# Even and odd blocks in two halves: the overlap-add of a block convolution with three additions instead of five, one PSUM pool, and channel pairs side by side

## The chip, the cores and the metric

The kernel runs on one core of one Trainium2 chip. The metric is the time of one execution on the device in microseconds (us). Three runs of the kernel before gave 13579.16, 13577.97 and 13587.48 us; their median is 13579.16 us.

## What is computed

The input x holds 32 images of 128 channels and 32 x 32 pixels; an image read as a sequence has L = 1024 positions. Two residual layers follow each other. Only the front part of the first layer is touched here:

```python
u = group_norm(x).reshape(B, S, L)                  # B = 32, S = 128
h = jnp.einsum('bdl,de->ble', u, W_enc) + b_enc     # 1024 model channels
K = 2.0 * jnp.einsum('dn,dnl->dl', Cc * Bd, vand).real   # 64 taps per model channel
y = irfft(rfft(z, n) * rfft(K, n), n)[..., :L]      # z is h with axes swapped: a causal convolution
y = gelu(y + D[:, None] * z)
```

So each of the 1024 model channels of each image is encoded from 128 input channels, and then convolved along its 1024 positions with a filter of 64 taps that belongs to that channel (D is folded into the first tap). After that the first layer has a gated linear unit, a layer norm and a decoder, and the second layer a deformable convolution. Those later parts are one long block of the program; the change does not touch them.

## The kernel before

The program runs three parts in a row: a small table of filters (`ssm_kernel_table`), the encoder and convolution (`ssm_convolution`), and the main block (`main_block`). The convolution's result `y_d` goes to device memory and the main block reads it back.

`ssm_convolution` walks over 8 groups k of 128 model channels. For each k it calls `encode(k)` and then `convolve(k, z)`. The instructions of each engine stand in the order in which these functions call them (`manual_schedule`)[...].

**Encoding.** For each of the 32 images, `image(b, u)` makes two halves g of four position blocks (128 positions each). A half is four matmuls (L223) with a block of the normalised image `u` as the stationary operand and the encoder's weights as the moving one. Their results lie in a PSUM tile `psz` of one bank. One VectorE addition (L227) adds the bias and writes the half into `z[g]`, laid out as position, channel, block, image. The innermost run of that write is one element: neighbouring channels lie NB x B = 128 elements apart. `psz` has two buffers. For k = 0 the group norm of the images runs inside the same loop (`group_norm_steps`, L161 to L180), spread over ScalarE, TensorE and VectorE in steps; the loads, the storing of `u_d` (L250) and the encoding of image t-3 stand between them. For k > 0 the normalised images are loaded back from `u_d` (L236).

**Convolution.** A convolution with 64 taps of a 128-position block is a matmul with a banded table `toe` of 192 columns (TW). The result's positions stand in reverse: its first RW = 64 columns run over into the next block, the other 128 are the block itself. In `convolve` the stationary operand is the half i of `z` for one channel, 128 positions by 128 columns (4 blocks x 32 images); the result has these 128 block-image rows as partitions. Channels are taken in groups of 8 (`CG`), with one load of `toe` each (L281), and inside a group in quads of four (`QC`). For each quad and each half i there are

- four matmuls into a PSUM tile `psy` of two banks (L299),
- a ScalarE copy of the overlapping columns into `t` (L307),
- VectorE additions that carry the overlap to the block that follows (L311): 64 rows and 32 rows inside the half, and for i = 1 another 32 rows that come from half 0, so five for the two halves,
- a ScalarE gelu that evacuates the tile into `yo` (L320).

The gelu of a tile isn't called at once: it goes on the list `waiting`, and `finish()` calls it after the next tile's copy and additions have been called. After the second quad of a group, `store` joins the same list: eight DMAs of 128 KB by GpSimd's queue (L332). The pool of `psy` has three buffers of two banks, and the group norm's small results take their tiles from that pool as well.

With blocks split into a first half (0 to 3) and a second half (4 to 7), ordered by `ORDER = (0, 2, 1, 3)`, the block that follows another one lies in the same half, except at one place. The order makes the carries contiguous in partitions.

```python
                        carry(64, 64, over[0:64])
                        carry(32, 32, over[64:96])
                        if i > 0:
                            carry(0, 32, last[96:P])
                        finish()
```

[...]two buffers of one bank and three of two are eight banks.

Of the kernel before, what the change touches and what calls it, by code (L numbers as in the profile page):

```python
# [7 lines left out]
F32 = mybir.dt.float32  # L8
AF = mybir.ActivationFunctionType
# [5 lines left out]
P = 128  # L15
# [10 lines left out]
TW = 192  # L26
# [3 lines left out]
CG = 8  # L30
# [130 lines left out]
def group_norm_steps(nc, pool, pm, gavg, eps, xt, out):  # L161


    s = pool.tile([P, 1], F32, tag="gn_s", name="gn_s")
    nm = pool.tile([P, 1], F32, tag="gn_m", name="gn_m")
    ss = pool.tile([P, 1], F32, tag="gn_ss", name="gn_ss")
    r = pool.tile([P, 1], F32, tag="gn_r", name="gn_r")
    nc.scalar.activation(out, xt, AF.Identity, accum_out=s)
    yield
    nc.tensor.matmul(pm[:, 0:1], gavg, s, start=True, stop=True)  # L170
    yield
    nc.scalar.mul(nm, pm[:, 0:1], -1.0)
    nc.scalar.activation(out, xt, AF.Square, bias=nm, accum_out=ss)
    yield
    nc.tensor.matmul(pm[:, 1:2], gavg, ss, start=True, stop=True)
    yield
    nc.scalar.activation(r, pm[:, 1:2], AF.Sqrt, bias=eps)
    nc.vector.reciprocal(r, r)
    nc.vector.tensor_scalar(out, xt, nm, r, op0=ALU.add, op1=ALU.mult)
    yield  # L180


def ssm_convolution(nc, tc, const, ins, x, u_d, kp_d, y_d):
# [12 lines left out]
    with tc.tile_pool(name="cvt", bufs=3) as tp, tc.tile_pool(  # L196
        name="cvz", bufs=1
    ) as zp, tc.tile_pool(name="cv1", bufs=1) as one, tc.tile_pool(
        name="cvu", bufs=5
    ) as up, tc.tile_pool(name="cvy", bufs=6) as yp, tc.tile_pool(  # L200
        name="cvg", bufs=4
    ) as gp, tc.tile_pool(
        name="cv_psz", bufs=2, space=PSUM
    ) as psz, tc.tile_pool(name="cv_psy", bufs=3, space=PSUM) as psy:
        w_enc = one.tile([P, D], F32, tag="w_enc", name="w_enc")
        nc.sync.dma_start(w_enc, ins["W_enc"])
        b_enc = one.tile([P, D], F32, tag="b_enc", name="b_enc")
        nc.sync.dma_start(b_enc, ins["b_enc_row"].to_broadcast([P, D]))

        def encode(k):  # L210

            z = [
                pool.tile([P, P, NB, B], F32, tag=f"z{g}", name=f"z_{k}_{g}")
                for g, pool in enumerate((one, zp))
            ]
            bias = b_enc[:, k * P : (k + 1) * P]

            def image(b, u):
                for g in range(2):
                    ps = psz.tile([P, NB, P], F32, tag="ps", name=f"psz_{k}_{b}_{g}")  # L220
                    for j in range(NB):
                        lo = (NB * g + ORDER[j]) * P
                        nc.tensor.matmul(  # L223
                            ps[:, j, :], u[:, lo : lo + P], w_enc[:, k * P : (k + 1) * P],
                            start=True, stop=True,
                        )
                    nc.vector.tensor_add(  # L227
                        z[g][:, :, :, b].rearrange("p d j -> p j d"),
                        ps,
                        bias[:, None, :].to_broadcast([P, NB, P]),  # L230
                    )

            if k > 0:
                for b in range(B):
                    u = up.tile([P, L], F32, tag="u", name=f"u_{k}_{b}")
                    nc.sync.dma_start(u, u_d[b])  # L236
                    image(b, u)
                return z


            running = {}

            def step(b):
                if b in running:
                    next(running[b][1])

            for t in range(B + 3):
                step(t - 2)
                if t - 2 in running:
                    nc.scalar.dma_start(u_d[t - 2], running[t - 2][0])  # L250
                step(t - 1)
                if t < B:
                    u = up.tile([P, L], F32, tag="u", name=f"u_{k}_{t}")
                    xt = yp.tile([P, L], F32, tag="yo", name=f"xt_{t}")
                    nc.sync.dma_start(xt, x[t])
                    pm = psy.tile([P, 2, 512], F32, tag="ps", name=f"gn_ps_{t}")
                    running[t] = u, group_norm_steps(
                        nc, gp, pm[:, 0, :2], const["gavg"], const["eps"], xt, u
                    )
                    step(t)  # L260
                if t >= 3:
                    image(t - 3, running.pop(t - 3)[0])
                step(t - 1)
                step(t)
            return z

        def convolve(k, z):
            rows = [t.rearrange("p d j b -> p d (j b)") for t in z]
            waiting = []

            def finish():
                for work in waiting:
                    work()
                waiting.clear()

            for g in range(P // CG):
                d0 = k * P + g * CG
                toe = tp.tile([P, CG, TW], F32, tag="toe", name=f"toe_{d0}")
                table = kp_d[d0 : d0 + CG, 0:TW]

                nc.sync.dma_start(  # L281
                    toe,
                    bass.AP(
                        tensor=table.tensor,
                        offset=table.offset,
                        ap=[[1, P], [KPW, CG], [1, TW]],
                    ),
                )
                yo = [
                    yp.tile([P, CG, P], F32, tag="yo", name=f"yo_{d0}_{i}") for i in range(2)  # L290
                ]
                for q in range(CG // QC):
                    c0 = q * QC
                    last = None
                    for i in range(2):
                        ps = psy.tile([P, 2, 512], F32, tag="ps", name=f"psy_{d0}_{q}_{i}")
                        ps = ps[:, :, : 2 * TW].rearrange("p h (c n) -> p h c n", c=2)
                        for c in range(QC):
                            nc.tensor.matmul(  # L299
                                ps[:, c // 2, c % 2, :],  # L300
                                rows[i][:, g * CG + c0 + c, :],
                                toe[:, c0 + c, :],
                                start=True,
                                stop=True,
                            )
                        over = tp.tile([P, 2, 2, RW], F32, tag=f"t{i}", name=f"t_{d0}_{q}_{i}")
                        nc.scalar.copy(over, ps[:, :, :, :RW])  # L307

                        def carry(to, rows, src):
                            own = ps[to : to + rows, :, :, P:TW]  # L310
                            nc.vector.tensor_add(own, own, src)  # L311

                        carry(64, 64, over[0:64])
                        carry(32, 32, over[64:96])
                        if i > 0:
                            carry(0, 32, last[96:P])
                        finish()

                        def gelu(to=yo[i][:, c0 : c0 + QC, :], ps=ps):
                            nc.scalar.activation(  # L320
                                to.rearrange("p (h c) l -> p h c l", c=2),
                                ps[:, :, :, RW:TW][:, :, :, ::-1],
                                AF.Gelu_apprx_tanh,
                            )

                        waiting.append(gelu)
                        last = over

                def store(yo=yo, d0=d0):
                    for i in range(2):  # L330
                        for j in range(NB):
                            nc.gpsimd.dma_start(  # L332
                                y_d[d0 : d0 + CG, :, i * NB + ORDER[j], :].rearrange(
                                    "d b l -> b d l"
                                ),
                                yo[i][j * B : (j + 1) * B],
                            )

                waiting.append(store)
            finish()  # L340


        with tc.manual_schedule():
            for k in range(KD):
                convolve(k, encode(k))


def deformable_general(nc, tc, const, ins, x1_d, out, image):
# [7 lines left out]
    with tc.tile_pool(name="gdf1", bufs=1) as one, tc.tile_pool(  # L356
# [27 lines left out]
        def prepare(b):  # L384
# [2 lines left out]
            nc.sync.dma_start(xt, x1_d[bass.ds(image, 1)].rearrange("o c l -> (o c) l"))  # L387
            v = one.tile([P, L], F32, tag="v", name=f"gen_dv_{b}")
            pm = psum.tile([P, 2], F32, tag="gn_ps", name="gn_ps")
            for _ in group_norm_steps(nc, one, pm, const["gavg"], const["eps"], xt, v):  # L390
                pass

            vT = two.tile([P, NCHUNK, C], F32, tag="vT", name=f"gen_dvT_{b}")
# [924 lines left out]
```

## Time and profile before

| | |
|---|---|
| runs (us) | 13577.97, 13579.16, 13587.48 |
| span of the profiled execution (us) | 13587.2 |
| TensorE busy, share of the span | 13106.8 us, 96% |
| VectorE / ScalarE / GpSimd busy | 65% / 24% / 67% |
| encoder and convolution, from the first image matmul to the last convolution matmul | about 31 to 1448 us of the span |

The times don't say which of the runs was profiled; the highest of them lies 0.3 us above the span. The encoder and convolution fill the first tenth of the span, and what follows is the main block. Within that tenth a group k takes some 168 us, of which about 75 us go to encoding and 94 us to the convolution; in k = 0, with the group norm, the encoding takes about 147 us.

The profile splits each fp32 matmul of the program into two matmul records with a weight load each, so the four matmuls of a tile are eight records. A record's duration [...]overlaps with its neighbours; what counts for throughput is the distance from start to start. In lists of groups, the columns are line, engine, operation, output and inputs, sizes, count, then busy time, mean duration in ns, the idle time of the engine before these instructions and what ended it.

### The profile page before, as it was taken

Reading aid. Unit: us, or ns where it says so; the run is one execution under the profiler, and the core shown is the slowest. Engines: PE = TensorE matmul, PEld = TensorE weight load, DVE = VectorE, ACT = ScalarE, POOL = GpSimd, SP = SyncE. Lnnn points to the kernel's source line nnn. Section 1 sums busy time; section 2 is a strip of 40 time slices with the busy share of each in tenths; the row PEclk is TensorE's granted clock in tenths of the full one; section 3 lists DMA queues with packets and bytes.
Section 4 is the critical chain, followed back from the end, with each engine's and each line's share of the span. In section 5 each row is a group of like instructions: output and inputs, shape, how many; then the busy total and the mean of one; then the engine's idle time right before and its main releaser. Section 6 shows DMA issues by size and latency. Waiting matters only on the chain.

```text
span 13587.2 us, 133930 instructions
## 1 busy us (share of the span) xinstructions
PE 13106.8 (96%) x40482; PEld 7248.5 (53%) x40482; DVE 8781.8 (65%) x12685; ACT 3291.8 (24%) x4767; POOL 9080.3 (67%) x8868
## 2 busy tenths in 40 slices
PE   7999899999999999999999999999999999999975
PEld 7888545555555555555555555555555555555533
DVE  7787226666666666666666666666666666666677
ACT  4333222222211122222222211112222222221145
POOL 2444227777777777777777777777777777777778
PEclk9999999999999999999999999999999999999988
DMA  7888428888888888888889888888888888988876
GB/s 244 275 277 273 132 90 231 234 239 236 231 227 231 233 235 238 238 236 232 230 234 239 235 229 229 231 232 237 238 237 236 232 230 235 240 235 231 230 198 175
DMA packets 1715626, 3105.77 MB, mean 229 GB/s; under 512 B 308306, under 2 KB 1018322, under 8 KB 1713874
## 3 DMA queue, kind: packets, MB, share of 16 engines
q1 hardware_dynamic: 1502290, 2641.91, 73.2%
q10 hardware_dynamic: 163456, 320.92, 6.6%
q0 software_dynamic: 49152, 134.28, 2.9%
q8 instruction: 329, 5.39, 0.2%
q14 instruction: 399, 3.27, 0.1%
HBM read 2630.36 MB, written 466.06 MB: 228 GB/s over the span
## 4 chain that ended last, share of the span: by engine, by line
PE 81%; DMA 9%; DVE 4%; ACT 2%; POOL 2%; issue 1%; SPq 1%; ACTq 0%; DVEq 0%; POOLq 0%
PE gpv L780 24%; PE gpg L757 23%; PE dps L1091 23%; DMA ds<-dhat 4%; PE gph L796 3%; PE gpo L685 3%; PE psy L299 3%; PE psz L223 2%; DMA y_d<-yo 2%; DMA dhat<-dh 2%; DVE z L227 1%; DVE ds L1048 1%; DMA dhy<-dhat 1%; POOL y_d L332 1%; ACT ds L1040 0%
## 5 line engine op out<-in xcount | busy, mean ns | idle before, releaser
L1094 DVE TENSOR_TENSOR dp<-dps,k_weight_slots 128x256 f32<-128x256 f32 (+17 forms) x6528 | 3087.1, 483 | 3109.5 <-PE dps L1091 2914.8
L1091 PE MATMUL dps<-ds,dxw 128*128 128x256 f32 (+18 forms) x13056 | 4701.1, 447 | 223.5 <-DVE ds L1048 177.5
L1116 POOL TENSOR_TENSOR dacc<-dacc,dp 128x256 f32<-128x256 f32 (+3 forms) x4736 | 4417.4, 933 | 396.5 <-DVE dp L1111 26.6
L1091 PEld LDWEIGHTS dps<-ds,dxw 128*128 128x128 f32 x13056 | 2472.7, 192 | 3203.6 <-issue 2537.5
L757 PE MATMUL gpg<-gy,g_w_glu 128*128 128x512 f32 x8192 | 3986.4, 593 | 23.5 <-DMA gy<-y_d 15.7
L780 PE MATMUL gpv<-gy,g_w_glu 128*128 128x512 f32 x8192 | 3975.7, 592 | 0.0
L1111 POOL TENSOR_TENSOR dp<-dp 128x448 f32<-128x448 f32 (+2 forms) x2142 | 2675.1, 1249 | 1882.1 <-DVE dp L1094 1879.4
L1048 DVE TENSOR_TENSOR ds<-ds,dhy 128x1024 f32<-128x1024 f32 (+3 forms) x2176 | 3148.6, 1447 | 762.4 <-DMA ds<-dhat 647.9
L757 PEld LDWEIGHTS gpg<-gy,g_w_glu 128*128 128x128 f32 x8192 | 1546.9, 190 | 1235.8 <-issue 964.9
L780 PEld LDWEIGHTS gpv<-gy,g_w_glu 128*128 128x128 f32 x8192 | 1551.7, 190 | 1155.3 <-issue 913.8
L818 POOL TENSOR_TENSOR gs<-gs,gq 128x512 f32<-128x512 f32 x448 | 628.5, 1403 | 1341.3 <-ACT gq L817 1341.3
L817 ACT ACTIVATE gq<-gr 128x512 f32<-128x512 f32 x448 | 282.3, 630 | 4673.6 <-DVE gr L809 4611.2
L332 POOL DMA_DIRECT2D y_d<-yo x1024 | 590.1, 583 | 869.7 <-ACT yo L320 699.2
L764 ACT ACTIVATE gs<-gpg,k_b_glu 128x512 f32<-128x512 f32 x512 | 351.8, 687 | 2488.0 <-PE gpg L757 2377.6
L953 ACT ACTIVATE dh<-dr,k_minus 128x624 f32<-128x624 f32 x768 | 621.7, 809 | 642.5 <-DMA dhat<-dh 563.1
L299 PE MATMUL psy<-toe,z 128*128 128x192 f32 x4096 | 704.7, 333 | 45.2 <-ACT yo L320 43.8
L299 PEld LDWEIGHTS psy<-toe,z 128*128 128x128 f32 x4096 | 667.5, 192 | 81.6 <-ACT yo L320 74.5
L311 DVE TENSOR_TENSOR psy<-psy,t 32x256 f32<-32x256 f32 (+1 forms) x1280 | 553.7, 433 | 204.7 <-ACT t L307 162.6
L788 DVE SCALAR_TENSOR_TENSOR gs<-gpv,k_b_glu,gs 128x512 f32<-128x512 f32 x512 | 379.7, 742 | 437.3 <-PE gpv L780 437.2
L687 POOL TENSOR_TENSOR gs<-gs,gr 128x512 f32<-128x512 f32 x448 | 634.7, 1417 | 0.0
L954 ACT ACTIVATE dh<-dh,one 128x624 f32<-128x624 f32 x768 | 626.3, 815 | 25.0
L223 PE MATMUL psz<-w_enc,u 128*128 128x128 f32 x4096 | 568.6, 293 | 44.9 <-DVE z L227 32.3
(162 smaller groups left out, 6052.4 us busy)
## 6 DMA issues: line engine op xcount, KB each, us to landing
dhy<-dhat SPq DMA_DIRECT2D x1536, 512.0 KB
ds<-dhat SPq DMA_DIRECT2D x1440, 512.0 KB
dhat<-dh ACTq DMA_DIRECT2D x768, 312.0 KB
y_d<-yo POOLq DMA_DIRECT2D x1024, 128.0 KB, 5.4
gy<-y_d SPq DMA_DIRECT2D x512, 256.0 KB
u<-u_d SPq DMA_DIRECT2D x224, 512.0 KB
toe<-kp_d SPq DMA_DIRECT2D x128, 768.0 KB
dxw<-dvt_d SPq DMA_DIRECT2D x1248, 64.0 KB
```

The source lines that it names most:

```text
L223: nc.tensor.matmul(ps[:, j, :], u[:, lo : lo + P], w_enc[:, k * P : (k + 1) * P], start=True, stop=True,)
L299: nc.tensor.matmul(ps[:, c // 2, c % 2, :], rows[i][:, g * CG + c0 + c, :], toe[:, c0 + c, :], start=True, stop=True,)
L332: nc.gpsimd.dma_start(y_d[d0 : d0 + CG, :, i * NB + ORDER[j], :].rearrange("d b l -> b d l"), yo[i][j * B : (j + 1) * B],)
L687: nc.gpsimd.tensor_add(sums[0], sums[0], r)
L757: nc.tensor.matmul(gate, w_glu[:, k, D + m * P : D + m * P + P], ys[k], start=(k == 0), stop=(k == KD - 1),)
L780: nc.tensor.matmul(val, w_glu[:, k, m * P : m * P + P], ys[k], start=(k == 0), stop=(k == KD - 1),)
L818: nc.gpsimd.tensor_add(sums[1], sums[1], sq)
L1048: nc.vector.tensor_mul(s[:, :m], s[:, :m], hy[:, :m])
L1091: nc.tensor.matmul(ps, xw[:, j, :], s[:, :m, :, y0 : y0 + ny], start=True, stop=True)
L1094: nc.vector.tensor_mul(prod[:, :m, :, y0 : y0 + ny], ps, w[:, :, :, None].to_broadcast([P, m, KY2, ny]),)
L1111: adder.tensor_add(prod[:, :m, 0], prod[:, :m, 0], prod[:, :m, 1])
L1116: nc.gpsimd.tensor_add(to, to, prod[:, slot : slot + nj, 0])
```

## The change

The blocks are split in another way: half 0 has the even blocks and half 1 the odd ones (`block(g, j) = 2 * ORDER[j] + g`). The block that follows an even block is then the odd one on the same partition in the other half, so one addition over all 128 partitions carries half 0 into half 1. Half 1 is carried to the next even block by additions of 64 and 32 rows. These are three additions for a quad. Both halves of a quad are therefore multiplied and copied first, then the three additions follow, and then `finish()`; the gelus of both halves are one entry of the list `waiting`.

The two PSUM pools become one, with four buffers of two banks. An image's two encoded halves lie in the two banks of one such tile (`both[:, g]`); the group norm takes a tile of its own for each of its two results per image.

`z[g]` is laid out as position, channel pair, block, image, channel of the pair: two channels lie side by side, and pairs lie 256 elements apart. The stationary operand of the convolution thus reads every second element. `store` writes to the rearranged block numbers.

```diff
-    nc.tensor.matmul(pm[:, 0:1], gavg, s, start=True, stop=True)
+    p = pm(0)
+    nc.tensor.matmul(p, gavg, s, start=True, stop=True)
...
-    ) as gp, tc.tile_pool(
-        name="cv_psz", bufs=2, space=PSUM
-    ) as psz, tc.tile_pool(name="cv_psy", bufs=3, space=PSUM) as psy:
+    ) as gp, tc.tile_pool(name="cv_ps", bufs=4, space=PSUM) as psum:
+
+        def banks(name):
+            return psum.tile([P, 2, 512], F32, tag="ps", name=name)
...
+        def block(g, j):
+
+            return 2 * ORDER[j] + g
...
-                pool.tile([P, P, NB, B], F32, tag=f"z{g}", name=f"z_{k}_{g}")
+                pool.tile([P, P // 2, NB, B, 2], F32, tag=f"z{g}", name=f"z_{k}_{g}")
...
             def image(b, u):
+                both = banks(f"psz_{k}_{b}")
                 for g in range(2):
-                    ps = psz.tile([P, NB, P], F32, tag="ps", name=f"psz_{k}_{b}_{g}")
+                    ps = both[:, g].rearrange("p (j d) -> p j d", j=NB)
                     for j in range(NB):
-                        lo = (NB * g + ORDER[j]) * P
+                        lo = block(g, j) * P
...
                     nc.vector.tensor_add(
-                        z[g][:, :, :, b].rearrange("p d j -> p j d"),
-                        ps,
-                        bias[:, None, :].to_broadcast([P, NB, P]),
+                        z[g][:, :, :, b, :].rearrange("p d j e -> p j d e"),
+                        ps.rearrange("p j (d e) -> p j d e", e=2),
+                        bias.rearrange("p (d e) -> p d e", e=2)[:, None].to_broadcast(
+                            [P, NB, P // 2, 2]
+                        ),
                     )
...
-                    pm = psy.tile([P, 2, 512], F32, tag="ps", name=f"gn_ps_{t}")
+                    def pm(n, t=t):
+                        return banks(f"gn_ps_{t}_{n}")[:, 0, 0:1]
...
-                    last = None
+                    out, over = [], []
                     for i in range(2):
-                        ps = psy.tile([P, 2, 512], F32, tag="ps", name=f"psy_{d0}_{q}_{i}")
+                        ps = banks(f"psy_{d0}_{q}_{i}")
...
-                                rows[i][:, g * CG + c0 + c, :],
+                                rows[i][:, (g * CG + c0 + c) // 2, c % 2, :],
...
-                        over = tp.tile([P, 2, 2, RW], F32, tag=f"t{i}", name=f"t_{d0}_{q}_{i}")
-                        nc.scalar.copy(over, ps[:, :, :, :RW])
-
-                        def carry(to, rows, src):
-                            own = ps[to : to + rows, :, :, P:TW]
-                            nc.vector.tensor_add(own, own, src)
-
-                        carry(64, 64, over[0:64])
-                        carry(32, 32, over[64:96])
-                        if i > 0:
-                            carry(0, 32, last[96:P])
-                        finish()
-
-                        def gelu(to=yo[i][:, c0 : c0 + QC, :], ps=ps):
+                        t = tp.tile([P, 2, 2, RW], F32, tag=f"t{i}", name=f"t_{d0}_{q}_{i}")
+                        nc.scalar.copy(t, ps[:, :, :, :RW])
+                        out.append(ps)
+                        over.append(t)
+
+                    def carry(to, rows, ps, src):
+                        own = ps[to : to + rows, :, :, P:TW]
+                        nc.vector.tensor_add(own, own, src)
+
+                    carry(0, P, out[1], over[0])
+                    carry(64, 64, out[0], over[1][0:64])
+                    carry(32, 32, out[0], over[1][64:96])
+                    finish()
+
+                    def gelu(yo=yo, c0=c0, out=out):
+                        for to, ps in zip(yo, out):
                             nc.scalar.activation(
...
-                        waiting.append(gelu)
-                        last = over
+                    waiting.append(gelu)
...
-                                y_d[d0 : d0 + CG, :, i * NB + ORDER[j], :].rearrange(
+                                y_d[d0 : d0 + CG, :, block(i, j), :].rearrange(
```

## The prediction

> **What bounds the kernel now.** I read the page first, for the place of the change. The chain that ended last gives its two matmul lines, psy L299 and psz L223, 3% and 2% of the span; the rest of the span is the main block, which isn't touched. So I cut the first 1450 us into stages by the lines of TensorE's matmuls. Two neighbouring stages of the view of busy time by stretch, one encoding and one convolution (start:end, length, then busy time and instructions of PE, PEld, DVE, ACT, POOL, then granted clock, DMA share, GB/s):
>
> ```profile
> 609.60:683.80 74.20, 68.83 (x513) 61.36 (x512) 65.72 (x67) 1.84 (x4) 10.21 (x18) 1.00 0.84 258
> 683.80:775.20 91.40, 86.83 (x513) 82.50 (x514) 68.68 (x158) 55.51 (x124) 63.08 (x110) 1.00 0.90 297
> ```
>
> Seven such encodings have a mean of 74.6 us, eight convolutions one of 93.5 us; the first encoding, with the group norm, takes 147 us (31 to 178). TensorE looks busy in both, so the next question is what it waits for. From the groups, by form, of 0 to 2000 us:
>
> ```profile
> L227 DVE TENSOR_TENSOR z<-psz,b_enc 128x512 f32<-128x512 f32 x512 | 516.2, 1041 | 89.9 <-PE psz L223 77.9 <-DMA kp_d<-kp 5.2
> ...
> L311 DVE TENSOR_TENSOR psy<-psy,t 32x256 f32<-32x256 f32 x768 | 327.0, 426 | 26.3
> ...
> L311 DVE TENSOR_TENSOR psy<-psy,t 64x256 f32<-64x256 f32 x512 | 226.6, 443 | 178.5 <-ACT t L307 162.6
> ```
>
> and from the waits of the same stretch:
>
> ```profile
> PEld psz L223 <- DVE z L227: 86.6, 243, 2.6
> ...
> PEld psy L299 <- ACT yo L320: 74.5, 125, 4.0
> ```
>
> Encoding: TensorE waits for the additions. The timeline shows one image:
>
> ```profile
> 641.49 2.03 DVE L227 TENSOR_TENSOR z<-psz,b_enc 128x512 f32<-128x512 f32 x2 [0.27 <-PE psz L223]
> ...
> 642.58 1.96 PEld L223 LDWEIGHTS psz<-w_enc,u 128*128 128x128 f32 x16 [0.33 <-DVE z L227]
> 643.77 2.04 DVE L227 TENSOR_TENSOR z<-psz,b_enc 128x512 f32<-128x512 f32 x2 [0.26 <-PE psz L223]
> 644.87 0.19 PEld L223 LDWEIGHTS psz<-w_enc,u 128*128 128x128 f32 x1 [0.33 <-DVE z L227]
> ```
>
> Loads start at 642.58, the first half's addition at 643.77 (1.19 later), it takes 1.04, and 0.05 after it the next image's loads start: 2.29 us an image, and 32 x 2.29 = 73 us. The second half's eight records run under the first addition.
>
> Convolution: eight records a tile at 0.162 us from start to start, 1.30 us a tile, 64 tiles 83 us; the other 10 us are DMA (share 0.90; gelu waits 51.6 us for the stores of `yo`). The end of a convolution shows the latency from TensorE to ScalarE and back:
>
> ```profile
> 1446.69 1.46 PE L299 MATMUL psy<-toe,z 128*128 128x192 f32 x8
> ...
> 1448.25 0.37 ACT L307 COPY t<-psy 128x256 f32<-128x256 f32 x1 [0.20 <-PE psy L299]
> 1448.52 0.60 ACT L320 ACTIVATE yo<-psy 128x512 f32<-128x512 f32 x1
> ```
>
> Matmuls end at 1448.15, the copy starts 0.10 later, and the gelu called after it ends at 1449.12. A waiting load starts 0.05 after the gelu that frees its buffer (another spot: gelu 571.29 + 0.60, load 571.94). With three buffers, tile n waits for the gelu of n-3, which stands behind the copy of n-2: its end, 1.0 us after the matmuls of n-2, falls inside the 1.30 us of the matmuls of n-1. That is why this loop hardly stalls today.
>
> **What the Trainium skill says.** "TensorE: Matmul & The Clock Gate", the table at its head: ScalarE's and VectorE's queues are strict FIFO. The trace agrees: each gelu stands behind the copy called before it. The same page, "What's actually happening": the clock is gated by activity in windows of about 3.4 us. The trace agrees: in the first encoding it halves for 3.41 or 6.83 us, after windows with 1.92 and 1.99 us of TensorE work, and not after ones with 2.12 and 2.17. "SBUF — State Buffer", Specifications: lines of 16 bytes, of which two hits are needed for full bandwidth. The trace has one side of this only: L227, writing single 4-byte elements 512 bytes apart, takes 1041 ns, while L717, as large and reading PSUM too, but writing in a row, takes 680.
>
> **The change, part by part.**
>
> 1. *L227 writes pairs.* No row shows pairs. Bounds: 680 ns (nothing left of the penalty) and 1041 (all left). I take 690, since two hits a line is what the page asks for.
>
> 2. *Both halves of an image in one PSUM tile.* In the built program, the second half's first matmul waits for the addition of the first half of the same image; it had no such wait before, since the halves were tiles of their own. The next image's first half waits for no addition. So the addition that ran under the second half's matmuls now stands between the halves. Counting from the stalled start of a second half: 16 loads take 1.96 (second half, then the next image's first), the addition starts 0.21 after the last load's end (the eighth ends near 0.98, its addition starts at 1.19), takes 0.69, and 0.05 later the next second half starts: 1.96 + 0.21 + 0.69 + 0.05 = 2.91 us an image, 93.1 us a group against 74.6. Seven groups: 7 x 18.5 = **+130 us**. The faster addition is what keeps it there; at 1.04 it would be 3.26.
>
> 3. *First encoding.* Its period of some 4.1 us runs sqrt, reciprocal, normalise, the DMA issue of `u_d` on ScalarE, mean, square; image t-3 stands before the second group-norm matmul on TensorE, and with a halved clock is on the chain already (16 records, 3.6 us). Now about 1 us (0.21 + 0.69 + 0.05) is inserted there. It counts where the clock is low, about a third of the images (mean clock 0.84), and a little elsewhere: **+15 us**, between 0 and 32. The shorter additions give nothing: the reciprocal already starts as soon as its sqrt ends.
>
> 4. *Convolution in pairs.* ScalarE's order becomes copy (q,0), copy (q,1), gelu (q-1,0), gelu (q-1,1). Four buffers hold two quads, so the matmuls of (q+1,0) wait for gelu (q-1,0), and that stands behind copy (q,1), which waits for the matmuls of (q,1): for everything TensorE has left. So TensorE empties once a quad. From above: 1448.15 to 1449.12 to the load, 0.97 + 0.05, plus 0.16 (the next matmul would have started that long before the end), plus 0.10 for a cold restart = 1.28 us. Gelu (q-1,1) ends 0.6 later, inside the matmuls of (q+1,0), and costs nothing. Quad: 16 x 0.162 + 1.28 = 3.88 us. A group has 32; the first two find buffers free: 30 x 3.88 + 2 x 2.60 = 121.6, and 1.3 at the next encoding's first tile, 122.9 against 93.5. Eight groups: 8 x 29.4 = **+235 us**. DMA no longer limits: 16.8 MB of stores and 12.6 MB of `toe` in 123 us are 239 GB/s, below the 297 moved above.
>
> 5. *Two additions fewer.* Five (3 x 426 + 2 x 443 = 2.16 us a quad) become three (about 1.31). VectorE isn't what TensorE or the gelu waits for: the quad's additions end some 1.4 us after copy (q,1), and their gelus come a quad later. Gain: 0. Without that cover, it would be at most 0.85 x 256 = 218 us.
>
> 6. *`z` read with a step of 8 bytes as weights.* Not in the trace. At best nothing: two elements still share a 16-byte line, and a load takes 0.107 us of the 0.162 between matmuls. If the load doubled to 0.213, it would be 0.051 x 16 x 256 = +209 us. I take 0.
>
> The store's rearranged blocks are the same number and size of DMAs: 0. The main block is the same program, started later.
>
> Sum: 130 + 15 + 235 = 380, on the profiled execution's span of 13587 us: 13967. The median of the runs lies 8 us below that execution, so 13579 + 380 = **13959 us**.
>
> **The rivals.**
>
> - *Pairs don't speed up L227* (1041 stays): 0.35 x 224 = +78, 14037. For it: nothing in this trace has runs of two. Against it: the page.
> - *The clock.* Encoding now has its longest pause, 0.78 us, between two stretches of 2.13, so the emptiest 3.41 us window has 2.13 us of work, close above the 1.99 that halved the clock. If it goes down as in the first encoding (0.84), 2.13/0.84 - 2.13 = 0.41 x 224 = +91: 14050. The convolution's pause of 1.0 us leaves 2.4 and is safer.
> - *Weights at half speed:* 14168, as above.
> - *The waits don't bite*, the other side: TensorE goes at its own pace, 16 x 0.111 x 32 = 57 us an encoding (58 by DMA: 16.8 MB at 290 GB/s), convolutions stay at 93.5: 7 x (58 - 74.6) = -116, 13463. It needs both hand-offs under other work; at 58 us the encoding could pay for at most 116/248 = 0.47 us of stall a quad, while copy and gelu alone take 0.87. The FIFO order speaks against it.
>
> **How the numbers follow.** My forecast 0.62; unpaired speed 0.12; clock 0.13; weights 0.08; waits that don't bite 0.03; stalls much smaller than I count, still slower, 0.02. The forecast alone spreads over 13900 to 14015 (stall 1.1 to 1.5 us: -45 to +55). Taking in the unpaired and clock cases and part of both goes to 14110; below, a margin to 13870. Faster by over 0.2% (27 us, about what a measurement of this kernel can tell from no change) 0.03, within it 0.01, slower 0.96.
>
> **What would show it.** Encodings of 93 us and convolutions of 123; TensorE's loads of psz waiting for the encoder's addition (L236 of the changed kernel) once an image, about 0.9 us before each second half; its loads of psy waiting for the gelu once a quad, 1.0 us or more, 240 times; that addition near 690 ns; clock 1.00 in both stages; the DMA share of convolutions down to about 0.75. I'm wrong if convolutions stay under 100 us, if weight loads of psy take longer than 190 ns, or if the time moved in the main block.

## The result and the profile after

The changed kernel takes 13984.12 us (median of four runs, 13978.99 to 13995.50) against 13583.32 us before: a ratio of 1.0293, with a 95% interval of 1.0279 to 1.0308. It is slower by 401 us; 13959 was forecast. The profiled execution took 13986.41 us, with a span of 13984.7 us.

All but some 3 us of it lies where the change was made. Stages cut by TensorE's first and last matmul of each line (us):

| | before | after | difference | forecast |
|---|---|---|---|---|
| first encoding, with the group norm | 146.8 | 165.4 | +18.6 | +15 |
| seven encodings, mean | 74.5 | 93.5 | 7 x 19.0 = +133 | +130 |
| eight convolutions, mean | 93.6 | 123.1 | 8 x 29.5 = +236 | +235, with the hand-off to the next encoding |
| between the stages | | | +6 | in the line above |
| after the last convolution | 12139.0 | 12142.4 | +3 | 0 |

Two neighbouring stages of the changed kernel, in the view of busy time by stretch (start:end, length, busy time and instructions of PE, PEld, DVE, ACT, POOL, then granted clock, DMA share, GB/s):

```profile
543.00:635.10 92.10, 66.19 (x513) 59.91 (x514) 44.44 (x65) 1.57 (x3) 5.59 (x10) 1.00 0.62 198
634.90:757.70 122.80, 91.68 (x514) 82.75 (x513) 41.10 (x94) 53.18 (x123) 67.01 (x117) 1.00 0.79 227
```

Before, weight loads (the second pair) filled 61.36 of 74.20 us and 82.50 of 91.40; their busy time is the same now, in longer stretches. DMA's share fell from 0.84 and 0.90 to 0.62 and 0.79. No engine is busy for as large a share of the stage as before: the engines wait for each other.

The groups by form, 0 to 2000 us, that answer to those shown of before:

```profile
L236 DVE TENSOR_TENSOR z<-psz,b_enc 128x512 f32<-128x512 f32 x512 | 354.3, 692 | 426.0 <-PE psz L232 420.6 <-DMA kp_d<-kp 5.4
...
L327 DVE TENSOR_TENSOR psy<-psy,t 64x256 f32<-64x256 f32 x256 | 113.3, 443 | 3.5
L327 DVE TENSOR_TENSOR psy<-psy,t 128x256 f32<-128x256 f32 x256 | 110.7, 433 | 646.6 <-ACT t L321 646.6
L327 DVE TENSOR_TENSOR psy<-psy,t 32x256 f32<-32x256 f32 x256 | 109.6, 428 | 8.7
```

The encoder's addition fell from 1041 to 692 ns, and the carries from 553.7 (327.0 and 226.6, rounded) to 333.6 us in all. VectorE is 383.7 us less busy over the span, and the kernel is slower: what it saved was not on the path. The waits of the same stretch (total, times, longest) say what is:

```profile
PEld psy L313 <- ACT yo L336: 319.2, 240, 2.7
PEld psz L232 <- DVE z L236: 269.6, 263, 7.6
```

Before, these were 74.5 and 86.6 us. There are 240 waits for the gelu: 8 groups of 30 quads. The timeline of two images, and of a quad (a row joins instructions that follow each other without a pause; PEld are TensorE's weight loads):

```profile
560.21 1.86 PEld L232 LDWEIGHTS psz<-w_enc,u 128*128 128x128 f32 x16 [0.97 <-DVE z L236]
560.21 2.05 PE L232 MATMUL psz<-w_enc,u 128*128 128x128 f32 x16 [0.78 <-DVE z L236]
...
561.41 0.69 DVE L236 TENSOR_TENSOR z<-psz,b_enc 128x512 f32<-128x512 f32 x1 [1.25 <-PE psz L232]
562.30 0.69 DVE L236 TENSOR_TENSOR z<-psz,b_enc 128x512 f32<-128x512 f32 x1 [0.20 <-PE psz L232]
563.04 1.86 PEld L232 LDWEIGHTS psz<-w_enc,u 128*128 128x128 f32 x16 [0.97 <-DVE z L236]
```

```profile
499.94 2.88 PE L313 MATMUL psy<-toe,z 128*128 128x192 f32 x16 [1.02 <-ACT yo L336]
...
502.90 0.37 ACT L321 COPY t<-psy 128x256 f32<-128x256 f32 x1 [0.93 <-PE psy L313]
503.17 1.09 ACT L336 ACTIVATE yo<-psy 128x512 f32<-128x512 f32 x2
503.31 1.35 DVE L327 TENSOR_TENSOR psy<-psy,t 128x256 f32<-128x256 f32 x3 [2.54 <-ACT t L321]
503.83 2.43 PEld L313 LDWEIGHTS psy<-toe,z 128*128 128x128 f32 x15 [1.30 <-ACT yo L336]
```

In the first, sixteen records (the second half of one image and the first half of the next) run through; the first half's addition runs from 562.30 to 562.99, and only then does the next second half start: 2.83 us an image. In the second, TensorE ends at 502.82, the copy of half 1 follows, then the older quad's first gelu, and the matmuls go on after it: 3.89 us a quad, of which TensorE's matmul row is empty for 1.02.

### The profile page after: what moved, and what is told of

Same layout as the page of the kernel before. It is cut to its first block, busy times and chain, and to the rows that moved or that the text cites. A ratio compares the mean times of both kernels' runs of the same rounds, so it can differ in the third digit from the quotient of the medians.

```text
span 13984.7 us, 133449 instructions
## 1 busy us (share of the span) xinstructions
PE 13142.2 (94%) x40482; PEld 7244.7 (52%) x40482; DVE 8398.1 (60%) x12173; ACT 3285.6 (23%) x4767; POOL 9091.4 (65%) x8868
## 4 chain that ended last, share of the span: by engine, by line
PE 82%; DMA 8%; DVE 3%; ACT 3%; POOL 1%; issue 1%; SPq 1%; ACTq 0%; DVEq 0%; POOLq 0%
PE gpv L799 23%; PE gpg L776 23%; PE dps L1110 22%; DMA ds<-dhat 5%; PE psy L313 4%; PE psz L232 4%; PE gph L815 3%; PE gpo L704 3%; DVE z L236 1%; DMA y_d<-yo 1%; DMA dhat<-dh 1%; ACT yo L336 1%; DVE ds L1067 1%; DMA dhy<-dhat 1%; ACT ds L1059 1%
## 5 line engine op out<-in xcount | busy, mean ns | idle before, releaser
L313 PE MATMUL psy<-toe,z 128*128 128x192 f32 x4096 | 734.8, 333 | 250.0 <-ACT yo L336 250.0
L313 PEld LDWEIGHTS psy<-toe,z 128*128 128x128 f32 x4096 | 664.3, 197 | 319.2 <-ACT yo L336 319.2
L327 DVE TENSOR_TENSOR psy<-psy,t 128x256 f32<-128x256 f32 (+2 forms) x768 | 333.7, 434 | 658.8 <-ACT t L321 646.6
L232 PEld LDWEIGHTS psz<-w_enc,u 128*128 128x128 f32 x4096 | 523.9, 206 | 278.7 <-DVE z L236 269.6
```

The source lines that it names most:

```text
L232: nc.tensor.matmul(ps[:, j, :], u[:, lo : lo + P], w_enc[:, k * P : (k + 1) * P], start=True, stop=True,)
L313: nc.tensor.matmul(ps[:, c // 2, c % 2, :], rows[i][:, (g * CG + c0 + c) // 2, c % 2, :], toe[:, c0 + c, :], start=True, stop=True,)
```

## Experiments

The theory: two hand-offs, one in each stage, account for the loss, and each is a matter of order and of tiles, not of the layout of z or of the additions. The rivals: the pairs slow the weights; the additions or the shared pool cost something; DMA limits the stages anyway. The kernel before was measured again beside the experiments, 13580.76 us in the first round (to the pairs alone) and 13580.31 in the second; the ratios, with their 95% intervals, use these.

### Each half in a tile of its own

```diff
-                both = banks(f"psz_{k}_{b}")
                 for g in range(2):
-                    ps = both[:, g].rearrange("p (j d) -> p j d", j=NB)
+                    ps = banks(f"psz_{k}_{b}_{g}")[:, 0].rearrange("p (j d) -> p j d", j=NB)
```

> The changed kernel, with each encoded half in a PSUM tile of its own (the first bank of it), from the same pool of four. Theory (the wait between the halves of an image costs what was predicted): the load of the second half no longer waits for the addition of the first; TensorE's pace decides, 16 x 0.111 plus about 0.1 = 1.9 us an image, encodings of about 60 us in place of 93.5, the first one back near 147 from 165; 7 x 33.5 + 18 = 252 us less than the changed kernel, about 13730; convolutions stay at 123. Rival (encoding is slow for another reason, such as the pairs' layout or the deeper shared pool): encodings stay above 85, and the time within 60 us of the changed kernel's 13984.

Measured: 13727.89 us, 256 less than the changed kernel; ratio to the kernel before 1.0105 (1.0088 to 1.0122). Encodings have a mean of 60.7 us, the first one 142.7, convolutions 123.1. One encoding of this kernel:

```profile
854.60:914.30 59.70, 58.13 (x513) 57.59 (x514) 44.39 (x65) 1.50 (x3) 5.50 (x10) 1.00 0.89 294
```

PE and PEld are busy for 58 of 59.7 us: TensorE's own pace. The wait between the halves is the encodings' loss, and without it an encoding takes 14 us less than in the kernel before, where the slower addition set the pace. The two halves never touched the same bank; the built program made the second half's matmuls wait for the first half's addition because both were views of one tile. The weight loads of that encoding's start show what is left:

```profile
854.57 0.97 PEld L231 LDWEIGHTS psz<-w_enc,u 128*128 128x128 f32 x8 [1.30 <-ACT yo L335]
856.51 0.97 PEld L231 LDWEIGHTS psz<-w_enc,u 128*128 128x128 f32 x8 [0.97 <-DVE z L235]
858.46 5.70 PEld L231 LDWEIGHTS psz<-w_enc,u 128*128 128x128 f32 x49 [0.97 <-DVE z L235]
```

Each of the seven later encodings has two such waits at its start, where the changed kernel waits for every image; why these two stay was not tested.

### The gelus by half

The gelu of the older quad's half 0 is called between the two copies:

```diff
+                        if i == 0 and waiting:
+                            waiting.pop(0)()
...
-                    def gelu(yo=yo, c0=c0, out=out):
-                        for to, ps in zip(yo, out):
+                    for to, ps in zip(yo, out):
+
+                        def gelu(to=to, c0=c0, ps=ps):
...
-                    waiting.append(gelu)
+                        waiting.append(gelu)
```

> The changed kernel, with the gelu of the previous quad's half 0 called right after the copy of half 0, and that of half 1 after the copy of half 1. Theory (the convolution's loss is ScalarE's order, which lets TensorE empty once a quad): no wait of 1.0 us for the gelu is left, convolutions return to between 84 (TensorE's own) and 94 (as before, limited by DMA), 236 us less than the changed kernel at 94: about 13750; encodings stay at 93.5. Rival (the loss is in the matmuls or additions themselves: weights read with a step of 8 bytes, or additions waiting for both copies): convolutions stay above 110 and the time above 13880.

Measured: 13746.91 us, 237 less than the changed kernel; ratio to the kernel before 1.0119 (1.0102 to 1.0136). Convolutions 93.3 us, encodings 93.8. The timeline of this kernel, with the order that was asked for:

```profile
960.86 0.37 ACT L321 COPY t<-psy 128x256 f32<-128x256 f32 x1 [0.42 <-PE psy L313]
961.13 0.60 ACT L339 ACTIVATE yo<-psy 128x512 f32<-128x512 f32 x1
961.26 1.35 DVE L329 TENSOR_TENSOR psy<-psy,t 128x256 f32<-128x256 f32 x3 [1.45 <-ACT t L321]
962.16 0.37 ACT L321 COPY t<-psy 128x256 f32<-128x256 f32 x1 [0.43 <-PE psy L313]
```

A gelu now ends inside the other half's matmuls. The additions still wait for both copies, and that, which the rival had named as a possible cause, costs nothing that shows: the convolutions are as short as before the change (93.6).

### Both

> Both edits in one kernel: halves in tiles of their own, and the gelus by half. Theory (two separate losses that add up): 252 + 236 us less than the changed kernel, about 13495, which is below the kernel before (13583), since encodings gain from the faster addition what the wait hid. Rival (DMA is the limit once TensorE runs on: 46 MB a group at about 297 GB/s are 155 us, where the two stages would take 60 + 94 = 154): part of the gain is lost again, 13520 to 13570.

Measured: 13501.61 us (13493.73 to 13516.14), 483 less than the changed kernel where the two alone gave 256 + 237 = 493; ratio to the kernel before 0.9937 (0.9920 to 0.9953). So the losses add up, nearly. A convolution and an encoding of this kernel:

```profile
805.90:898.10 92.20, 88.06 (x514) 82.73 (x513) 41.10 (x94) 55.67 (x124) 62.90 (x110) 1.00 0.93 301
898.00:960.10 62.10, 58.75 (x514) 57.75 (x514) 44.92 (x66) 1.96 (x4) 10.92 (x20) 1.00 0.91 301
```

Encodings are 63.0 us here in the mean, 2.3 more than with the first edit alone. The rival put such a remainder down to DMA, but DMA's share and rate in an encoding are about the same in both kernels (0.91 and 301 GB/s here, 0.89 and 294 there). The loads at this encoding's start show another cause:

```profile
898.03 0.97 PEld L231 LDWEIGHTS psz<-w_enc,u 128*128 128x128 f32 x8 [0.22 <-ACT yo L338]
900.72 0.97 PEld L231 LDWEIGHTS psz<-w_enc,u 128*128 128x128 f32 x8 [1.73 <-DVE z L235]
902.67 0.97 PEld L231 LDWEIGHTS psz<-w_enc,u 128*128 128x128 f32 x8 [0.97 <-DVE z L235]
904.61 3.54 PEld L231 LDWEIGHTS psz<-w_enc,u 128*128 128x128 f32 x31 [0.97 <-DVE z L235]
```

There are three waits for the encoder's addition in place of two, and the added one takes 1.45 to 1.92 us in the seven encodings. What is left, some 0.6 us, was not taken apart further.

### Pairs alone, in the kernel before

```diff
-                pool.tile([P, P, NB, B], F32, tag=f"z{g}", name=f"z_{k}_{g}")
+                pool.tile([P, P // 2, NB, B, 2], F32, tag=f"z{g}", name=f"z_{k}_{g}")
...
-                        z[g][:, :, :, b].rearrange("p d j -> p j d"),
-                        ps,
-                        bias[:, None, :].to_broadcast([P, NB, P]),
+                        z[g][:, :, :, b, :].rearrange("p d j e -> p j d e"),
+                        ps.rearrange("p j (d e) -> p j d e", e=2),
+                        bias.rearrange("p (d e) -> p d e", e=2)[:, None].to_broadcast(
+                            [P, NB, P // 2, 2]
+                        ),
...
-            rows = [t.rearrange("p d j b -> p d (j b)") for t in z]
+            rows = [t.rearrange("p d j b e -> p d e (j b)") for t in z]
...
-                                rows[i][:, g * CG + c0 + c, :],
+                                rows[i][:, (g * CG + c0 + c) // 2, c % 2, :],
```

> The kernel before, with only the layout of z changed to pairs of channels: first and second halves, five additions, two PSUM pools as before. Theory (pairs cut the addition from 1.04 to 0.69 us and cost nothing as weights): an image takes 1.19 + 0.69 + 0.05 = 1.93 us in place of 2.29, encodings 62 in place of 74.5, 7 x 12.7 = 89 us less than the kernel before: about 13494; convolutions stay at 93.6. Rival (weights with a step of 8 bytes cost something, which the changed kernel's stalls covered): convolutions get longer by up to 26 us each, and the time lies at or above that of the kernel before.

Measured: 13495.26 us (13487.34 to 13500.98), 85 less than the kernel before; ratio 0.9932 (0.9916 to 0.9949). Encodings 63.9 us in place of 74.5; convolutions 92.5. This is one edit of the change, and of the kernels here that compute everything it has the lowest median; the runs of the kernel with both edits overlap with it, so even and odd halves, three additions and four buffers add nothing measurable on top.

### The changed kernel without pairs

> The changed kernel with z in the layout of before (one channel at a time, 512 bytes apart). Theory: each addition is back at 1041 ns, and since it stands between the halves of an image, all 0.35 us of it are on TensorE's path: 3.2 us an image in place of 2.83, 7 x 32 x 0.35 = 78 us more and some in the first encoding: 14060 to 14075; convolutions stay at 123. Rival (weights with a step of 8 bytes cost something in the changed kernel): convolutions get shorter than 122, and the time is below 14040.

The edit is the one just shown, backwards. Measured: 14084.20 us, ratio to the kernel before 1.0369 (1.0352 to 1.0387), 100 more than the changed kernel and somewhat more than expected. Encodings are 105.3 us. Once an encoding is under way an image takes 3.16 us, 0.33 more than the 2.83 of the changed kernel, as the addition between the halves takes some 1.02 us in place of 0.69. The mean of 105.3 also holds the start, where both halves wait, and 6.8 us of half clock in each of the seven encodings. The first encoding takes 176.0 us, 10.6 more than in the changed kernel. Convolutions run at 122.56 us, where the changed kernel's convolutions at full clock run at 122.73, so reading the weights with a step of 8 bytes costs under 0.2 us of 123.

### Five additions

The kernel with both edits, with the five additions of before:

```diff
-            return 2 * ORDER[j] + g
+            return NB * g + ORDER[j]
...
-                    carry(0, P, out[1], over[0])
-                    carry(64, 64, out[0], over[1][0:64])
-                    carry(32, 32, out[0], over[1][64:96])
+                    for i in range(2):
+                        carry(64, 64, out[i], over[i][0:64])
+                        carry(32, 32, out[i], over[i][64:96])
+                    carry(0, 32, out[1], over[0][96:P])
```

> The kernel with both edits (halves in tiles of their own, gelus by half), but with first and second halves and five additions a quad as before. Theory (VectorE's additions are under TensorE's work and DMA; their number doesn't matter): as with three, 13502 within 20 us, VectorE's busy time 218 us higher. Rival (the three additions of the even and odd halves are worth something once the waits are gone): 40 us or more slower than 13502.

Measured: 13504.63 us (13495.48 to 13529.09), ratio to the kernel before 0.9940 (0.9923 to 0.9956): no difference to three additions (13501.61) that can be told from noise. What the change is named for, fewer overlap additions, is worth nothing here once the hand-offs are gone; five additions with the hand-offs in place were not run.

### Quads of channels

The changed kernel with four channels side by side (`e=4` in place of `e=2`), so that the weights are read with a step of 16 bytes.

> The changed kernel with four channels side by side in place of two, so that the weights are read with a step of 16 bytes, one element to a 16-byte line. By the line rule of the Trainium skill (SBUF page) the loads of psy should get slower: if a load doubles to 0.21 us, convolutions get 26 us longer each, about 14190. Rival (a weight load doesn't feel the step): convolutions stay at 123 and the time at 13984 within 20; the addition at 690 ns or a little less in both.

Measured: 14305.06 us, ratio to the kernel before 1.0530 (1.0513 to 1.0548), 321 more than the changed kernel. Encodings as in the changed kernel, 92.0 undisturbed, with the addition at 691 ns; convolutions 162. The convolution's line in this kernel (durations in ns, min/median/max), and the same line of the changed kernel after it:

```profile
L313 PEld LDWEIGHTS psy<-toe,z x4096: 307/330/338, 197.8 to 2165.6; 128*128 128x128 f32 x196
```

```profile
L313 PEld LDWEIGHTS psy<-toe,z x4096: 193/197/337, 196.6 to 1841.8; 128*128 128x128 f32 x196
```

A record's load takes 330 ns, against 197 with pairs and 190 in the kernel before, and matmuls follow each other at 0.233 us in place of 0.162: 0.071 x 16 x 256 = 291 us of the 321. The rest fits the clock, whose mean is 0.98 in these convolutions and 0.96 in the seven later encodings. The loads agree with the line rule of the Trainium skill ("SBUF — State Buffer", Specifications), here for weights: two elements to a 16-byte line are nearly free, one is not. The load alone did double, as I had allowed for: where a second load follows the first at once, after a wait, it starts 0.212 us later, against 0.108 with adjacent elements and 0.116 with pairs. The pace of 0.233 lies above that; why was not tested. So 0.116 hides under the 0.162 from matmul to matmul, and 0.212 doesn't. Of the three steps that were run, pairs are the one that serves both sides: enough for the addition, not too much for the weights.

### Half of the banded table

> The kernel with both edits, which leaves out every second load of the banded table (odd groups use the table of the even group before them, so their results are those of other filters): 6.3 MB less of some 46 MB for each group of 128 channels. Theory (with both waits gone the convolutions of 94 us are limited by DMA, TensorE alone needs 83): convolutions fall to 84 to 87 us, encodings to 60 to 62, about 70 us less than 13502: 13430. Rival (something else holds them at 94, such as the gelu's hand-off): convolutions stay above 91.

This kernel leaves out every second load of `toe`, so what it computes belongs to other filters; only its time is of use. Measured: 13471.09 us (13463.73 to 13484.35), 31 less than the kernel with both edits, not 70. Convolutions fall from 93.9 to 89.0 us, at a DMA share of 0.83:

```profile
786.10:874.70 88.60, 86.83 (x514) 82.81 (x513) 41.11 (x94) 55.75 (x124) 65.54 (x114) 1.00 0.83 246
```

DMA is part of what keeps convolutions above TensorE's 83 us, but a cut of 6.3 MB in 46 gave back under half of it, and encodings didn't change (63.1). The waits from 190 to 1300 us, first with both edits, then with half of the table as well, show the other part:

```profile
PEld psy L312 <- ACT yo L338: 74.6, 150, 2.8
ACT yo L338 <- DMA y_d<-yo: 57.4, 46, 2.9
```

```profile
PEld psy L313 <- ACT yo L339: 40.5, 128, 2.7
ACT yo L339 <- DMA y_d<-yo: 17.8, 15, 2.8
```

ScalarE's waits for the stores of `yo` fall from 46 to 15. Of TensorE's waits for a gelu, 128 remain, most of them short (the median is 0.22 us): a hand-off that DMA has no part in. In the 7.5 convolutions of this stretch the 40.5 us are 5.4 a convolution, nearly all of the 6 us above 83; some 2.4 of them (17.8 us in all) fit the waits for stores.

## Why the prediction was right

By its steps:

1. *The addition in pairs.* 690 was taken between 680 and 1041; it is 692.
2. *Both halves in one tile.* Forecast 2.91 us an image and 93.1 an encoding; it is 2.83 and 92.1 where the clock stays at 1.00, and 93.5 in the mean. The sixteen loads take 1.86 in place of 1.96, since only one of the two tiles restarts after a wait. The cause is shown by taking it away. At the start of each encoding both halves wait, not only the second (three blocks of eight loads, 1.94 us apart); the sum did not have that.
3. *First encoding.* Forecast +15, measured +18.6, and with the halves apart it is gone (142.7). The inserted wait is there; that the granted clock would also sink (mean 0.84 before, 0.74 after) was not in the sum, and the two were not separated.
4. *Quads.* Forecast 3.88 us a quad and 121.6 a convolution, 122.9 with the hand-off to the next encoding; measured 3.89, 122.7 and 123.8. 240 waits, as counted. Reordering two calls removes them.
5. *Two additions fewer:* nothing, shown with five additions once the hand-offs are gone.
6. *Weights with a step of 8 bytes:* nothing, shown by the kernel without pairs. One of the signs of being wrong did appear: loads of psy take 197 ns, more than 190. The sign was drawn too tight, as the 7 ns stay under the pace of the matmuls.

The clock was a rival with a chance of 0.13. In encodings under way it did not come, but the sign "clock 1.00 in both stages" failed: it halved at the start of three of the seven later encodings and cost 4.0 + 4.9 + 1.6 = 10.5 us over the undisturbed 92.05. At the start both halves wait, so there is less work in a stretch of time, and what decides is where the windows of 3.41 us fall. A record's duration overlaps with its neighbours; to count work, take for each record the distance from start to start in a stream instead (0.111 us in encodings, 0.162 in convolutions, nothing for the group norm's one-column matmuls). Counted so, the windows ahead of the three falls hold 1.31 us each. The emptiest window after which the clock stayed full holds 1.39, and in an encoding under way none holds less than 1.78. The first of the falls:

```profile
327.60:337.90 10.30, 8.73 (x40) 8.13 (x38) 2.77 (x4) 0.00 (x0) 2.55 (x5) 0.50 0.70 204
```

The spans of the two profiled executions differ by 397.5 us, 17 more than the sum: 4 in the first encoding, 3 in the other seven (10 of the clock, less 7 because an undisturbed one is 1 us shorter than forecast), 7 in the convolutions and their edges (the first of them is 3 us longer than the others), 3 in the main block. That the clock and the shorter image nearly cancel is luck; the forecast had neither. The rival of waits that don't bite asked for two hand-offs under other work; the trace shows each of them in full, image by image and quad by quad.

One reading in it was too simple, though the sum didn't rest on it: that the 10 us by which convolutions before stood above TensorE's 83 us "are DMA". Of the 125 waits for a gelu (74.5 us) in that kernel, ScalarE's own waits for stores explain 34 (51.6 us), about two thirds of the time; the others are short. So that loop did stall a little. The halved table, in another kernel, gave back 5 of some 11 us.

## What to carry to other kernels

A pool's depth counts in units of what is handed back together: four buffers that are filled and released two by two, with the release queued behind the newest tile's evacuation, let the producer run dry once a round (240 waits, 319.2 us), where the same four released one by one, and three before, did not. Ask of each wait what stands ahead of its releaser in that engine's queue. And two results that share one tile can share its dependencies, so put into one tile only what is produced and consumed together; a saving on an engine that others don't wait for (here 384 us of VectorE) is no saving.

## What the runs showed of the hardware

- VectorE's addition of 128x512 from PSUM into SBUF takes 1041 ns with single 4-byte elements 512 bytes apart, 692 with runs of two, 691 with runs of four: the second element of a run is the whole gain.
- TensorE's weight load of 128x128 fp32 takes 190 ns a record with adjacent elements, 197 with a step of 8 bytes and 330 with 16. From one load to the next, with nothing between, it is 108, 116 and 212 ns. At 16 bytes matmuls follow each other at 0.233 us in place of 0.162.
- TensorE's granted clock halved at the start of encodings with no pause of the matmuls over 1.02 us. In the ten traces, up to the last convolution, all 137 falls follow a window of 3.41 us with at most 1.38 us of matmul work, counted as above by distances from start to start; of the 4072 windows after which it stayed full, 18 hold as little. By the records' durations no such line comes out: a window with 1.85 us kept the clock in the changed kernel, and windows with 2.12 lost it with four channels side by side.
- From the end of the matmuls to a waiting copy on ScalarE it takes 0.08 to 0.10 us, and from the end of the gelu or the addition that frees a buffer to TensorE's waiting load 0.05.
